# A masked two-layer attention kernel: moving the first batch's count, the last but one batch's units and statistics, and the last products and stores

## The chip, the core and the metric

The kernel runs on one core of a Trainium2 chip. A core has five engines with their own instruction queues: TensorE (PE, matrix products; PEld is its loading of weights), VectorE (DVE), ScalarE (ACT), GpSimd (POOL) and SyncE (SP), which here only issues transfers. The metric is the device time of one execution in microseconds (us).

## The reference

Sixteen graphs of 1024 nodes with 256 features pass two layers of masked multi-head attention, each behind a normalization without weights and a ReLU, and each with a residual. The first layer has 4 heads of 64, the second 8 heads of 32.

```python
# x: (16, 1024, 256) float32, adj: (16, 1024, 1024) int32 of 0 and 1
h = jnp.maximum(_layernorm(x, axis=-1), 0.0)
x = x + _L0_gnn_ref(h, adj, Wq, Wk, Wv, Wo, bo)     # H = 4, DK = 64
h = jnp.maximum(_layernorm(x, axis=-1), 0.0)
x = x + _L1_gnn_ref(h, adj, Wq, bq, Wk, bk, Wv, bv, Wo, bo)   # H = 8, D = 32

# in a layer
scores = jnp.einsum('bhne,bhme->bhnm', Q, K) * scale
scores = jnp.where(mask, scores, -jnp.inf)
attn = jax.nn.softmax(scores, axis=-1)
heads = jnp.einsum('bhnm,bhme->bhne', attn, V)
concat = heads.transpose(0, 2, 1, 3).reshape(...)
return concat @ Wo.T + bo
```

## The kernel before

**Steps.** Scores are computed transposed: keys on the partitions, queries along the free axis. A *step* handles four blocks of 128 keys by 512 queries. Its pieces are `scores` (L457, four products into two PSUM pairs `ps`), `exponentials` (for each pair of blocks L480 on DVE, which brings in the mask, and L486 on ACT, the exponential), and `weigh` (L498, products of the exponentials `p` with the values, gathered in `po`). A *group* is half of the heads for one half of the queries (`qh` 0 or 1, `g` 0 or 1): 4 steps in layer 0, 8 in layer 1. A batch so has 16 steps in layer 0 and 32 in layer 1, and there are 768 in all. The order is layer 0 of batch 0, and then always layer 0 of batch b+1 followed by layer 1 of batch b; at the end stands layer 1 of the last batch. Below, `a` is the first step of a batch's layer 0, `c` the first step of the layer 1 that follows it (for the last but one batch step 704), and `e` = `c` + 32 the first step of the last batch's layer 1.

**The stream.** `Stream.run` walks the steps, two at a time in layer 0 and one at a time in layer 1. `weigh` of a step comes two steps after its scores (`LEAD`). All other work is put at a step with `later(step, function, ...)`. Within a step the order is: the scores, `weigh`, the counts, the exponentials, then what is due there in the order in which it was put, and last the *units*, which are large pieces of TensorE work. They are `k` and `q` (L273), `values` (L309) and `end_half` (L439), sixteen 256-column or eight 512-column instructions each. On an even step of layer 1 that has a unit, `weigh` is left to the next step:

```python
if wide == 2 or i % 2 or not self.large(i):
    for _, st in waiting:
        weigh(st)
```

Each engine runs its instructions in program order, so this walk is also the order in each queue.

**The sums of the softmax.** Sums over the keys are made by adding `p` tiles first and then multiplying with ones on TensorE (`count`, L350, into the one bank `pz`). In layer 0 `add_tiles` adds the tiles of two steps (L507 and L510 on DVE or POOL, L511 and L513 on POOL), and `count_added` counts at the end of the query half. In layer 1 POOL adds pairs of steps (L611), and some sums are added by transfers (L595). An odd step's `p` tile has only two buffers, an even one's seven; the reader that frees the odd ones is L510 or L611. `spread` copies the sums to SBUF (L369, ACT) and sends them with four transfers to `sums` (L382, SP). `invert` takes reciprocals (L390, DVE) and stores them (L392, SP). `fetch` reads them back spread out (L401, SP), and `normalize` scales `cat` with them (L409, POOL). `copy_out` (L361, ACT) has filled `cat` from `po`, and frees the one `po` bank. `end_half` multiplies `cat` with the output weights into `py` (L439) and adds the result to `x` (L444, DVE); in layer 1 it stores `x` as well (L447, SP). `test` (L295, DVE) folds the sums into a verdict on their range.

All of `ps`, `pq`, `pv` and `py` take turns in three PSUM pairs, so a product waits for the reader of the third one before it.

**The next layer's inputs.** `norms` puts `stats` at two steps (L198 and L199 on DVE; at the second of them also L202 to L208 on POOL), `norm` at two more (L217, ACT) and `add_bias` (L226, POOL). `block_inputs` puts `turn_blocks` (L243, DVE), a store (L248) and four loads (L255) on SP, and the units `k`, `q` and `values`.

**The end.** The very last group is in a hurry: `finish` scales the last half of the heads itself, in two halves of the queries (L420 and L421, DVE), multiplies (L424), adds (L430) and stores with eight transfers (L432, SP). Behind it stand the verdict (L838 to L842), its load into every engine (L1019) and a branch around a careful version that is not taken here (L1020).

Of the kernel before, what the change touches and what calls it, by code (L numbers as in the profile page):

```python
# [18 lines left out]
P = 128  # L19
# [71 lines left out]
def fast_program(ctx, tc, a, w, loads, chk):  # L91
# [3 lines left out]
    nc = tc.nc  # L95
    x, adj, out = a["x"], a["adj"], a["out"]
    B, N, E = x.shape
# [18 lines left out]
    def psum_pair(name):  # L116
        return ps_s.tile([P, 2, 512], F32, tag="ps_s", name=name)
# [3 lines left out]
    def quarters(of, b, half):  # L121

        rows = of[b].rearrange("(t h p g) e -> h g p t e", h=QH, p=32, g=4)[half]
        return [rows[g] for g in range(4)]

    def by_tile(cols):

        return cols.rearrange("p (g t q) -> p t g q", g=4, q=32)

    def tiled(cols):  # L130

        return cols.rearrange("p (t g q) -> p t g q", g=4, q=32)
# [186 lines left out]
    class Group:  # L319
# [91 lines left out]
        def finish(self):  # L411

            inp, qh = self.inp, self.qh
            inv = work.tile([P, 512], F32, tag="inv", name=f"inv_{self.n}")
            py = psum_pair(f"py_{self.n}").rearrange("p a (t e) -> p (a t) e", e=E)
            rows, cat = xs[inp.b, qh], self.half.cat
            dst = quarters(out, inp.b, qh)
            for h in range(2):
                q = ts(h, 256)
                nc.vector.reciprocal(tiled(inv)[:, ts(h, 2)], by_tile(self.s)[:, ts(h, 2)])  # L420
                nc.vector.tensor_mul(cat[:, self.g, q], cat[:, self.g, q], inv[:, q])  # L421
                for i in (2 * h, 2 * h + 1):
                    for c in range(2):
                        nc.tensor.matmul(  # L424
                            py[:, i, :], cat[:, c, ts(i, P)], w.o[self.layer][:, c, :],
                            start=(c == 0), stop=(c == 1),
                        )
            for h in range(2):
                t = ts(h, 2)
                nc.vector.tensor_add(rows[:, t, :], py[:, t, :], rows[:, t, :])  # L430
                for g in range(4):
                    nc.sync.dma_start(dst[g][:, t, :], rows[ts(g, 32), t, :])  # L432

        def end_half(self):
            inp, qh = self.inp, self.qh
# [88 lines left out]
    class Stream:  # L524
# [12 lines left out]
        def later(self, i, f, *args):  # L537
            self.due.setdefault(i, []).append((f, args))
# [101 lines left out]
        def end_group(self, i, gr):  # L640

            if gr.hurry:
                for f in (gr.spread, gr.finish, gr.inp.test):
                    self.later(i, f)
                return

            if gr.layer == 0:
                if gr.g == 0:
                    gr.half.first = gr
                    return  # L650
                self.later(i + 3, gr.count_added)
                at = (3, 4, 5, 7, 11) if gr.qh else (3, 5, 6, 7, 11)
                if gr.inp.b == B - 1 and gr.qh:
                    at = 3, 4, 5, 7, 13
                if gr.inp.b == 0:
                    at = (3, 5, 5, 6, 8) if gr.qh else (3, 5, 6, 7, 9)
            else:
                at = ((6, 12, 15, 19), (8, 12, 14, 17, 19), (6, 9, 11, 14), None)[2 * gr.qh + gr.g]
                if gr.pairs:
                    at = 2, 5, 6, 7, 9  # L660
                elif gr.last:
                    at = 4, 6, 7, 9, 11
            for k, f in zip(at, (gr.spread, gr.invert, gr.fetch, gr.normalize)):
                self.later(i + k, f)
            if gr.last:

                k = 7 if gr.layer or gr.inp.b == 0 else 25 if gr.inp.b == B - 1 else 37
                self.later(i + k, gr.inp.test)
            if gr.g == 1:
                self.later(i + at[4], gr.end_half)  # L670
# [79 lines left out]
    def norms(inp, half, *at, whole=False, bias=None):  # L750

        for i, f in zip(at, (inp.stats, inp.stats, inp.norm, inp.norm)):
            rest = (whole,) if i in at[2:] else ()
            later(i, f, half, (0, 1) if i in (at[0], at[2]) else (2, 3), *rest)
        later(at[3] + 1 if bias is None else bias, inp.add_bias, half)

    def half_inputs(inp, half, *at):

        for i, f in zip(at, (inp.turn, inp.k, inp.q, inp.values)):
            later(i, f, half)  # L760

    def block_inputs(inp, half, turn, put, place, *at):

        later(turn, inp.turn_blocks, half)
        later(put, inp.put_blocks, half)
        later(place, inp.place_blocks, half)
        for i, f in zip(at, (inp.k, inp.q, inp.values)):
            later(i, f, half)
# [9 lines left out]
    for t in range(NT):  # L778
        i = 7 + 2 * t
# [8 lines left out]
    for b in range(B - 1):  # L788
        mine, a, c = inputs[1][b], first[b + 1], second[b]
        if b == 0:  # L790

            norms(mine, 0, a + 4, a + 6, a + 7, a + 8, whole=True)
            half_inputs(mine, 0, a + 10, a + 12, a + 13, a + 14)
            norms(mine, 1, a + 10, a + 11, a + 12, a + 13, whole=True)
            half_inputs(mine, 1, a + 15, c, c + 6, c + 2)
        else:
            norms(mine, 0, a - 20, a - 16, a - 15, a - 13, bias=a)
            block_inputs(mine, 0, a - 10, a - 8, a - 4, a, a + 2, a + 8)
            norms(mine, 1, a - 14, a - 10, a - 8, a - 6, bias=a + 6)
            block_inputs(mine, 1, a, a + 6, a + 7, c, c + (6 if b + 2 < B else 8), c + 2)  # L800
        for i, u in zip((0, 2, 4, 6, 7, 9, 11, 13), range(NT)):
            later(a + i, masks[b].second, u)
        if b + 2 < B:
            other, mask = inputs[0][b + 2], masks[b + 2]
            later(a + 6, open_x, b + 2, 0)
            later(c, open_x, b + 2, 1)
            if b == 0:
                norms(other, 0, a + 12, a + 14, c, c + 1, bias=c + 34)
                block_inputs(other, 0, c + 2, c + 3, c + 4, c + 8, c + 16, c + 18)
                norms(other, 1, c + 3, c + 4, c + 6, c + 7, bias=c + 36)  # L810
                block_inputs(other, 1, c + 8, c + 9, c + 12, c + 22, c + 26, c + 30)
            else:
                norms(other, 0, a + 10, a + 12, a + 13, a + 15, bias=c + 34)
                block_inputs(other, 0, c, c + 1, c + 2, c + 8, c + 16, c + 18)
                norms(other, 1, c + 2, c + 4, c + 5, c + 6, bias=c + 36)
                block_inputs(other, 1, c + 7, c + 8, c + 12, c + 22, c + 26, c + 30)
            at = 5, 8, 10, 12, 14, 45, 49, 51, 53
            for t in range(NT):
                later(a + at[t], mask.load, t)
                later(a + at[t + 1], mask.put, t)  # L820
                later(a + at[t + 1] + (1 if t == 4 else 2), mask.flip, t)
        else:
            last, e = inputs[1][b + 1], c + 32
            norms(last, 0, c + 8, c + 10, c + 11, c + 12)
            block_inputs(last, 0, c + 14, c + 15, c + 16, c + 20, c + 22, c + 26)
            norms(last, 1, c + 18, c + 19, c + 20, c + 21)
            block_inputs(last, 1, c + 24, c + 25, c + 26, e, e + 8, e + 2)
            for i, u in zip((4, 8, 12, 16, 18, 20, 24, 28), range(NT)):
                later(c + i, masks[b + 1].second, u)
    stream.run()  # L830
# [156 lines left out]
def kernel(  # L987
# [28 lines left out]
    with ExitStack() as fast, tc.manual_schedule():  # L1016
        fast_program(fast, tc, a, w, loads, chk)
# [61 lines left out]
```

## Time and profile before

| | |
|---|---|
| Median of 3 runs | 3116.97 us (3116.34 to 3117.56) |
| The profiled execution's own time | 3117.3 us |
| Its span, first to last instruction | 3115.5 us |
| PE busy | 3092.8 us (99%), 16724 instructions |
| DVE busy | 2478.7 us (80%), 2754 |
| ACT busy | 2243.3 us (72%), 2440 |
| POOL busy | 2354.3 us (76%), 1358 |
| Mean granted clock of TensorE | 0.998 |
| L480, one instruction | 1215 ns, x1536 |
| L486, one instruction | 1056 ns, x1536 |
| L611, one instruction | 2428 ns, x510 |

Busy time is the sum over an engine's instructions, and the share is that of the span. A row of a timeline gives start, duration, engine, line, operation, what it writes and reads, and how many instructions were merged; in brackets follow the engine's idle time before it and the instruction that ended it. A row of the waits gives who waited for whom: us in total, times, longest. A row of busy time in a stretch gives the stretch, its length, the busy time of PE, PEld, DVE, ACT and POOL with instruction counts, the granted clock (1.00 is full speed), the share of the transfer engines and GB/s. Starts are us from the start of the span.

### The profile page before, as it was taken

Reading aid. Unit: us, or ns where it says so; the run is one execution under the profiler, and the core shown is the slowest. Engines: PE = TensorE matmul, PEld = TensorE weight load, DVE = VectorE, ACT = ScalarE, POOL = GpSimd, SP = SyncE. Lnnn points to the kernel's source line nnn. Section 1 sums busy time; section 2 is a strip of 40 time slices with the busy share of each in tenths; the row PEclk is TensorE's granted clock in tenths of the full one; section 3 lists DMA queues with packets and bytes.
Section 4 is the critical chain, followed back from the end, with each engine's and each line's share of the span. In section 5 each row is a group of like instructions: output and inputs, shape, how many; then the busy total and the mean of one; then the engine's idle time right before and its main releaser. Section 6 shows DMA issues by size and latency. Waiting matters only on the chain.

```text
span 3115.5 us, 45742 instructions
## 1 busy us (share of the span) xinstructions
PE 3092.8 (99%) x16724; PEld 1221.2 (39%) x16724; DVE 2478.7 (80%) x2754; ACT 2243.3 (72%) x2440; POOL 2354.3 (76%) x1358
## 2 busy tenths in 40 slices
PE   9999999999999999999999999999999999999998
PEld 4443433434334343433434434343343433434333
DVE  5778787887878888788887878878788787887776
ACT  6667767777677767777777677777777767776775
POOL 3568778787877868778687786877868788786876
PEclk9999999999999999999999999999999999999999
DMA  4224545454463544535445463554545545453331
GB/s 132 58 69 113 129 106 123 121 112 118 102 140 110 119 119 101 139 103 116 122 101 138 106 129 99 116 129 103 126 116 112 123 109 122 121 111 82 78 73 33
DMA packets 259224, 341.28 MB, mean 110 GB/s; under 512 B 58288, under 2 KB 218288, under 8 KB 241968
## 3 DMA queue, kind: packets, MB, share of 16 engines
q0 software_dynamic: 19152, 139.47, 22.8%
q1 hardware_dynamic: 239840, 198.82, 22.0%
q8 instruction: 133, 2.18, 0.3%
q14 instruction: 99, 0.81, 0.1%
HBM read 149.95 MB, written 47.96 MB: 64 GB/s over the span
## 4 chain that ended last, share of the span: by engine, by line
PE 94%; DVE 1%; SPq 1%; DMA 1%; ACT 1%; issue 1%; POOL 0%; ACTq 0%; DVEq 0%; POOLq 0%
PE ps L457 32%; PE po L498 29%; PE pq L273 14%; PE pv L309 7%; PE py L439 7%; PE pz L350 4%; DVE p L480 1%; SPq L382 0%; DMA sums<-s 0%; SPq L152 0%; DMA inv<-vd 0%; ACT p L486 0%; POOL p L611 0%; DVE x L444 0%; PE py L424 0%
## 5 line engine op out<-in xcount | busy, mean ns | idle before, releaser
L486 ACT ACTIVATE p<-p 128x1024 f32<-128x1024 f32 x1536 | 1614.2, 1056 | 663.0 <-DVE p L480 599.4
L480 DVE SCALAR_TENSOR_TENSOR p<-mask,ps 128x1024 f32<-128x1024 fp8e5 x1536 | 1787.5, 1215 | 379.4 <-PE ps L457 369.1
L611 POOL TENSOR_TENSOR p<-p,p 128x1024 f32<-128x1024 f32 x510 | 1212.6, 2428 | 176.8 <-PE po L498 176.7
L457 PE MATMUL ps<-qT,kT 32*128 32x512 f32 (+1 forms) x6144 | 1097.5, 628 | 3.9 <-DVE p L480 2.0
L498 PE MATMUL po<-p,v 128*32 128x512 f32 (+1 forms) x6144 | 978.6, 600 | 1.7 <-ACT cat L361 1.5
L457 PEld LDWEIGHTS ps<-qT,kT 32*128 32x128 f32 (+1 forms) x6144 | 371.0, 184 | 660.0 <-issue 313.8
L498 PEld LDWEIGHTS po<-p,v 128*32 128x32 f32 (+1 forms) x6144 | 233.4, 118 | 680.7 <-issue 486.6
L511 POOL TENSOR_TENSOR p<-p 128x1024 f32<-128x1024 f32 x128 | 302.6, 2364 | 142.2 <-DVE p L510 136.9
L510 POOL TENSOR_TENSOR p<-p,p 128x1024 f32<-128x1024 f32 x64 | 150.9, 2358 | 199.8 <-DVE p L507 179.6
L409 POOL TENSOR_TENSOR cat<-cat,inv 128x512 f32<-128x512 f32 x127 | 175.6, 1388 | 99.8 <-DMA inv<-vd 99.4
L439 PE MATMUL py<-wo,cat 128*128 128x256 f32 x1008 | 236.4, 388 | 2.7 <-POOL cat L409 1.5
L309 PE MATMUL pv<-wv,hT 128*128 128x256 f32 x1024 | 237.7, 385 | 0.0
L273 PE MATMUL pq<-hT,wk 128*128 128x512 f32 x512 | 236.7, 605 | 0.0
L273 PE MATMUL pq<-hT,wq 128*128 128x512 f32 x512 | 236.6, 605 | 0.0
L439 PEld LDWEIGHTS py<-wo,cat 128*128 128x128 f32 x1008 | 187.4, 191 | 77.8 <-issue 23.5
L309 PEld LDWEIGHTS pv<-wv,hT 128*128 128x128 f32 x1024 | 189.4, 190 | 71.7 <-issue 15.1
L507 DVE TENSOR_TENSOR p<-p 128x1024 f32<-128x1024 f32 x128 | 172.6, 1349 | 0.0
L595 POOL DMA_DIRECT2D p<-p x133 | 122.6, 922 | 55.4 <-POOL p L611 26.8
L350 PE MATMUL pz<-p,ones 128*32 128x512 f32 x1248 | 163.1, 596 | 0.0
L361 ACT COPY cat<-po 128x512 f32<-128x512 f32 x128 | 73.4, 573 | 116.7 <-PE py L439 96.6
L444 DVE TENSOR_TENSOR x<-py,x 128x1024 f32<-128x1024 f32 x63 | 77.2, 1225 | 99.7 <-PE py L439 98.8
L226 POOL TENSOR_TENSOR x<-x,bo 128x1024 f32<-128x1024 f32 x64 | 155.7, 2504 | 0.0
(52 smaller groups left out, 1667.2 us busy)
## 6 DMA issues: line engine op xcount, KB each, us to landing
p<-p POOLq DMA_DIRECT2D x133, 1024.0 KB, 7.8
adj<-in_adj_dram SPq DMA_DIRECT2D x512, 128.0 KB, 3.0
turned<-hn SPq DMA_DIRECT2D x58, 512.0 KB, 3.8
hT<-turned SPq DMA_DIRECT2D x232, 128.0 KB, 3.0
x<-in_x_dram SPq DMA_DIRECT2D x128, 128.0 KB, 3.0
inv<-vd SPq DMA_DIRECT2D x128, 128.0 KB, 3.0
inv<-vd SPq DMA_DIRECT2D x252, 64.0 KB, 3.0
out_dram<-x SPq DMA_DIRECT2D x124, 128.0 KB, 2.2
```

The source lines that it names most:

```text
L273: nc.tensor.matmul(pq[:, m, :], wt[self.layer][:, c, ts(m, P)], self.hT[half][:, c, :], start=(c == 0), stop=(c == 1),)
L309: nc.tensor.matmul(pv[:, i, :], self.hT[half][:, c, ts(i, P)], w.v[self.layer][:, c, :], start=(c == 0), stop=(c == 1),)
L350: nc.tensor.matmul(self.s[ts(r, 32), :], w.ones.to_broadcast([P, 32]), of, start=start, stop=stop)
L409: nc.gpsimd.tensor_mul(o, o, inv)
L439: nc.tensor.matmul(py[:, i, :], self.half.cat[:, c, ts(i, P)], w.o[self.layer][:, c, :], start=(c == 0), stop=(c == 1),)
L457: nc.tensor.matmul(st.ps[i // 2][:, i % 2, :], gr.inp.kT[r * D : (r + 1) * D, gr.g, ts(kt, P)], gr.inp.qT[gr.qh][r * D : (r + 1) * D, gr.g ...
L480: nc.vector.scalar_tensor_tensor(out=half, in0=gr.mask.m[gr.qh][:, kt // 4, :, kt % 4].unsqueeze(1).to_broadcast([P, 2, 512]), scalar=-EDG ...
L486: nc.scalar.activation(half, half, AF.Exp, scale=gr.scale)
L498: nc.tensor.matmul(gr.o[r * D : (r + 1) * D, :], gr.inp.v[:, kt, h * D : (h + 1) * D], st.halves[i // 2][:, i % 2, :], start=(kt == 0), st ...
L507: nc.vector.tensor_add(a, a, b)
L511: nc.gpsimd.tensor_add(a, a, b)
L611: nc.gpsimd.tensor_add(half, half, of)
```

## The change

Four things are edited, and the arithmetic stays the same.

1. In `finish` the four products with the first group's half of `cat` are issued ahead of the scaling of the second half; the products with the second half follow each scaling. The start and stop marks now stand on the first and the last product of a PSUM bank. Of the eight last stores every second one is issued by ACT.
2. In batch 0, layer 0, second query half: `count_added` and `spread` one step sooner, `invert` two steps, `fetch` and `normalize` one step. With steps taken in twos, `count_added`, `spread`, `invert` and `fetch` so move to the pair of steps before, and `normalize` stays in its pair (22 and 23), but on its first step, ahead of that pair's `add_tiles`. `end_half` stays.
3. In the layer 1 of the last but one batch: the `end_half` of the last batch's layer 0 moves from c+14 to c+18, and `q` of its own second half from c+8 to c+10.
4. For the last batch's layer 1: statistics of its first half from c+8 and c+10 to c+6 and c+8. Of its second half: statistics from c+18 and c+19 to c+20 and c+22, norm from c+20 and c+21 to c+23 and c+24 (`add_bias` with it from c+22 to c+25), turn, store and loads each two steps later, and `q` from e+8 to e+10.

```diff
@@ finish
+            def product(i, c):
+                nc.tensor.matmul(
+                    py[:, i, :], cat[:, c, ts(i, P)], w.o[self.layer][:, c, :],
+                    start=c == 0 and i % 2 == 0, stop=c == 1 and i % 2 == 1,
+                )
+
+            for i in range(4):
+                product(i, 0)
             for h in range(2):
                 q = ts(h, 256)
                 nc.vector.reciprocal(tiled(inv)[:, ts(h, 2)], by_tile(self.s)[:, ts(h, 2)])
                 nc.vector.tensor_mul(cat[:, self.g, q], cat[:, self.g, q], inv[:, q])
                 for i in (2 * h, 2 * h + 1):
-                    for c in range(2):
-                        nc.tensor.matmul(
-                            py[:, i, :], cat[:, c, ts(i, P)], w.o[self.layer][:, c, :],
-                            start=(c == 0), stop=(c == 1),
-                        )
+                    product(i, 1)
...
-                    nc.sync.dma_start(dst[g][:, t, :], rows[ts(g, 32), t, :])
+                    queue = nc.scalar if g % 2 else nc.sync
+                    queue.dma_start(dst[g][:, t, :], rows[ts(g, 32), t, :])
@@ end_group
-                self.later(i + 3, gr.count_added)
+                early = gr.inp.b == 0 and gr.qh
+                self.later(i + (2 if early else 3), gr.count_added)
                 at = (3, 4, 5, 7, 11) if gr.qh else (3, 5, 6, 7, 11)
                 if gr.inp.b == B - 1 and gr.qh:
-                    at = 3, 4, 5, 7, 13
+                    at = 3, 4, 5, 7, 17
                 if gr.inp.b == 0:
-                    at = (3, 5, 5, 6, 8) if gr.qh else (3, 5, 6, 7, 9)
+                    at = (2, 3, 4, 5, 8) if gr.qh else (3, 5, 6, 7, 9)
@@ the order of the work, b >= 1
-            block_inputs(mine, 1, a, a + 6, a + 7, c, c + (6 if b + 2 < B else 8), c + 2)
+            block_inputs(mine, 1, a, a + 6, a + 7, c, c + (6 if b + 2 < B else 10), c + 2)
...
-            norms(last, 0, c + 8, c + 10, c + 11, c + 12)
+            norms(last, 0, c + 6, c + 8, c + 11, c + 12)
             block_inputs(last, 0, c + 14, c + 15, c + 16, c + 20, c + 22, c + 26)
-            norms(last, 1, c + 18, c + 19, c + 20, c + 21)
-            block_inputs(last, 1, c + 24, c + 25, c + 26, e, e + 8, e + 2)
+            norms(last, 1, c + 20, c + 22, c + 23, c + 24)
+            block_inputs(last, 1, c + 26, c + 27, c + 28, e, e + 10, e + 2)
```

## The prediction

> **What bounds the kernel now.** I read the page first: TensorE (PE) is busy 3092.8 of 3115.5 us, so all that an edit of the order can win is PE's idle time, its slow clock, and the tail after the last matmul. Then I asked which waits PE has in the whole run:
>
> ```profile
> PE py L424 <- DVE cat L421: 2.3, 1, 2.3
> ...
> PE py L439 <- DVE p L480: 1.2, 1, 1.2
> ```
>
> The first is the tail's. The second lies at 2927 us, and near it lies most of what the lines left out hold of scores (L457) that wait for L480, 2.0 us in 6 waits, and of po (L498) for the copy L361, 1.5. Two waits of py on POOL's scaling (L409), 1.5 in all, are batch 0's, at 160 us. These are the three places of the change. Next the busy time in stretches of 3.41 us, laid on the two places where the granted clock is half:
>
> ```profile
> 2924.39:2927.80 3.41, 1.38 (x7) 0.49 (x6) 2.31 (x3) 3.41 (x6) 3.41 (x2) 0.99 0.30 60
> 2927.80:2931.22 3.42, 3.42 (x9) 2.71 (x9) 3.17 (x3) 2.96 (x3) 3.17 (x2) 0.51 0.02 5
> 2941.45:2944.87 3.42, 2.13 (x19) 0.47 (x17) 3.42 (x4) 3.42 (x5) 3.19 (x2) 1.00 0.54 153
> 3098.47:3101.88 3.41, 1.08 (x5) 0.67 (x4) 3.02 (x3) 0.27 (x1) 0.00 (x0) 0.99 0.03 2
> 3101.88:3105.29 3.41, 3.41 (x9) 2.67 (x9) 1.26 (x2) 0.00 (x0) 0.00 (x0) 0.51 0.00 0
> ```
>
> After the bounds come PE's busy us and, third from the right, the clock. Stretches with 1.38 and 1.08 us of PE are each followed by one at half clock; one with 2.13 is not (nor is one with 1.96 at 20 us). So a stall costs a second time. Last the timeline of each place.
>
> **The tail.**
>
> ```profile
> 3098.16 0.70 PE L424 MATMUL py<-wo,cat 128*128 128x256 f32 x2
> ...
> 3101.19 4.95 PE L424 MATMUL py<-wo,cat 128*128 128x256 f32 x14 [2.33 <-DVE cat L421]
> ...
> 3106.17 1.29 DVE L430 TENSOR_TENSOR x<-py,x 128x512 f32<-128x512 f32 x2 [3.00 <-PE py L424]
> ```
>
> and, from the answer on line 1020, the branch at the end:
>
> ```profile
> L1020 PEldq COMPARE_BRANCH  x1: 4455/4455/4455, 3109.3 to 3109.3; - x1
> ```
>
> Each product is two instructions of some 0.215 us at full clock (the 16 of L439 take 3.65 us: 0.23 each). The change issues all four first-group products (8 instructions) at 3098.16, until about 3100.05, in what was idle time. After the first scaling (3101.19) come 4 instructions, until 3102.1; the last 4 wait for the second scaling (ends 3103.18) and run 3103.29 to 3104.31. The stretch 3098.47 to 3101.88 then has 1.58 + 0.67 = 2.25 us of PE instead of 1.08, above the 2.13 that kept the clock, so I take no half clock: L430 starts at 3104.33 and not 3106.17, 1.84 sooner. If it stays at half, the last 4 take 1.9 us: 1.0 sooner. The Trainium skill (TensorE: Matmul & The Clock Gate, "Why this matters for your kernels") says that gaps over some 3 us are to be avoided; by that a gap of 2.33 is harmless, the 14 instructions would keep their 4.95 / 14 = 0.354 us, and the last 4 end at 3104.7: 1.45. The row of 0.51 decides: 1.84.
>
> Behind it SP issues 8 stores from 3106.89, 4.48 us in all, the last with 1.22; only then its load of the verdict (3111.4) and the waits for the stores. With four on ACT, idle there, each queue needs 4 x 0.43 = 1.7 us. No ACT-issued transfer is in the trace, so its cost is bounded by the same issue on SP (0.43, landing 1.7 to 4.1 us) and by one from POOL (0.92, landing 7.8); I take SP's, the same kind of issue. But L1020's branch on PE, started by the verdict at 3109.3, ends at 3113.71 whatever SP does, and the span ends 1.8 us later; SP's last wait is about 3114.5. So of SP's 2.8 us only some 0.75 comes out. The skill (DMA: Bandwidth & Descriptors, "Rules for kernel authors") holds that spreading over queues saves issue time only. Read alone that gives 4.48 - 1.7 = 2.8; the branch's row leaves 0.75. Tail: -1.84 - 0.75 = **-2.6** (-1.0 to -4.5; with ACT's landing at 7.8 the stores gain becomes a loss of about 1).
>
> **Batch 0** (steps 20 to 28):
>
> ```profile
> 153.91 2.37 POOL L510 TENSOR_TENSOR p<-p,p 128x1024 f32<-128x1024 f32 x1
> ...
> 156.31 2.35 DVE L480 SCALAR_TENSOR_TENSOR p<-mask,ps 128x1024 f32<-128x1024 fp8e5 x2 [0.85 <-POOL p L510]
> ...
> 164.58 1.22 DVE L444 TENSOR_TENSOR x<-py,x 128x1024 f32<-128x1024 f32 x1 [0.94 <-PE py L439]
> ```
>
> L510 frees the buffer that L480 of step 25 writes; the scaling of cat (L409, 2.51 us) came after it, at 158.70. The count (1.0 us of PE) moves from 139.58 to about 128.7; its sums are final at 124.0, so it waits for nothing, and PE's total at 144 is unchanged. The copy (0.59 on ACT), four sum transfers (2.4 on SP, behind an adjacency load that ends at 133), reciprocal (0.25), one store and four inverse loads (2.4, behind the next adjacency load) follow one pair of steps sooner and land near 150; the x load behind them on SP issues some 1.3 us later, for a batch that is not yet read. So the scaling is ready. It now stands ahead of L510 on POOL: 153.95 to 156.45. The products need not wait (0.94 + 0.53 = 1.47 of idle, with the issue around it 1.77: end 162.7). But L510 ends at 158.8, so L480 of step 25 starts there, 2.5 late. Two waits vanish behind it: L295 and L507 took 1.45 and 2.34 us while POOL scaled, 0.45 and 1.2 elsewhere. DVE: 158.85 + 2.35 + 0.45 + 1.2 + 1.25 = 164.1 for L444, against 164.58. The next scores' third block takes its PSUM buffer from L444 and then follows DVE, which has no idle time until 182.7. So 0.5 and not 1.77: **-0.5** (-1.8 if DVE catches up; +1.0 if L507 stays at 2.34).
>
> **Last but one batch.** c is its first layer-1 step (2874.21), e = c+32. Three rules from the rows: a step's scores take 1.07 us or end 1.16 after the first L480 of the step before (L480 ended 2918.23, scores 2919.39); an odd step's L480 waits for the POOL sum of the step four earlier:
>
> ```profile
> 2924.01 1.22 DVE L480 SCALAR_TENSOR_TENSOR p<-mask,ps 128x1024 f32<-128x1024 fp8e5 x1 [1.67 <-POOL p L611]
> ...
> 2927.61 5.41 PE L439 MATMUL py<-wo,cat 128*128 128x256 f32 x16 [1.19 <-DVE p L480]
> ...
> 2943.86 1.06 PE L498 MATMUL po<-p,v 128*32 128x512 f32 x8 [1.29 <-ACT cat L361]
> ```
>
> and a unit (8 or 16 matmuls, 3.65 us) on an even step defers that step's po products to the next. Followed through:
> - Statistics at c+6 put 1.31 us of DVE ahead of the L480 of c+7: scores of c+8 end at 2907.2, not 2905.84. Those at c+8 put another 1.31 ahead of c+9; q, now at c+10, runs 2913.3 to 2916.9. The scores of c+12 start at 2920.7 against 2917.75: 3.0 lost.
> - Their POOL part (1.9 us) now precedes the two scalings, which waited 1.83 for a transfer until 2912.87: ending at 2915.4, not 2914.1. It no longer stands at 2919.74 before L611. c+12 to c+17 have no unit now: scores of c+13 start at 2922.8, c+15 2927.5, c+17 2934.0. Before, c+17 started at 2938.80 with the 3.65 unit behind it: 2934.0 + 3.65 = 2937.65, 1.2 ahead.
> - Then POOL is late again: the sums of c+13 end at 2936.7 and 2939.1, L480 of c+17 waits for both, and py at c+18 starts at 2940.4 after 1.3 idle. The worst 3.41 us before it has about 2.0 of PE, near the 1.96 that kept the clock: no half clock, by a little. py ends 2944.0; the 1.29 wait for the copy (L361) is hidden under it. Scores of c+19 start 0.8 ahead of 2944.85.
> - The later statistics of half 1 free ACT at c+20, and the 0.26 that PE waited for L287 goes. Turn, store and four loads move two steps on SP, landing near 2986 for k at about 2988: covered by 2 us, and if not, at most 2 us are lost. add_bias at c+25 fits POOL's 3.06 of idle. q from e+8 to e+10 swaps equal steps: 0.
> - c+27's scores: 2973.2 against 2974.50. The same rules put the old ones at 2974.1, so I count the nearer **-1.0**. Bounds: +1.5 with a half clock at c+18 (1.76, partly swallowed as before), -2.8 if the 1.3 idle isn't there.
>
> **Sum**: -2.6 - 0.5 - 1.0 = -4.1 on the profiled 3117.3 gives 3113.2; the median of the runs is 0.3 lower, so 3112.9.
>
> **Rivals.** (1) *Each stall simply goes*: -3.4, -1.8, -2.8, together -8.0: 3109.0. For it: each wait named is the one moved. Against: DVE and POOL have no slack in two of the places. (2) *The gains are given back*: the clock stays half in the tail (-1.0), batch 0 and the stretch give 0: 3116.0. (3) *Slower: POOL's debt in the eight steps c+10 to c+18 without a unit*. Four pairs of sums (18.9) with two scalings (2.6), statistics (1.9), two accumulates (2.4) and a bias (2.5) are 28.3 us against four pairs of steps at 5.36 (21.4): 6.9 of debt, and the two odd-step buffers absorb one pair, 5.4. If more than that is uncovered, each pair costs as the worst one before, 2920.38 to 2932.95 less a unit: 8.9 against 5.4, 3.5 lost. Four such are 14, less the 5.5 lost there now, plus 1.8 of half clock: +10.3; with the tail and batch 0, +7.2: 3124.2.
>
> **Numbers.** 0.2% is 6.2 us, about what a measurement of this kernel can tell from no change. My forecast 0.62 (own range 3110.8 to 3115.0), rival 1 0.17, rival 2 0.15, rival 3 0.06. Faster is rival 1, same the forecast and rival 2, slower rival 3. The range 3109.0 to 3116.9 leaves out part of rival 1's far side and rival 3.
>
> **What would show it.** Tail: 8 instructions of py from 3098, the clock of the next 3.4 us full, L430 about 1.8 us after the second L421's start, four stores on each of SP and ACT. Batch 0: no py wait, L480 waiting some 3.3 us for L510. Last but one batch: py at c+18 with about 1.3 us of idle on L480. Wrong if the clock is half at c+18 or in the tail, if L444 in batch 0 is not where DVE stands, or if the end waits for a store from ACT.

## The result, and the profile after

The changed kernel is slower: a median of 3122.02 us (3120.50 to 3123.59 over 20 runs) beside 3116.32 us of the kernel before (3114.24 to 3118.64 over 20 runs). The ratio is 1.0018, with an interval of 1.0012 to 1.0025: 5.7 us more, where 4.1 less were forecast. The profiled execution of the changed kernel took 3121.75 us, and its span is 3120.0.

In the changed kernel the lines behind `finish` have a number 6 higher, and those behind `end_group` 7: L480 is now L486, L457 L463, L498 L504, L611 L617, L439 L445, and the branch L1020 is L1027. In `finish` itself L424, L421 and L430 became L420, L430 and L435. Lines up to L409, with the range test L295, kept theirs.

First the page, then PE's waits in the whole run (who waited for whom: us in total, times, longest):

```profile
span 3120.0 us, 45743 instructions
...
PE 3097.7 (99%) x16724; PEld 1220.7 (39%) x16724; DVE 2481.5 (80%) x2754; ACT 2243.8 (72%) x2440; POOL 2351.5 (75%) x1358
```

```profile
PE ps L463 <- DVE p L486: 5.8, 8, 1.8
...
PE py L420 <- DVE cat L430: 1.9, 2, 1.0
...
PE py L445 <- DVE p L486: 1.2, 1, 1.2
```

PE has the same 16724 instructions as before and 4.9 us more of busy time, which with the same work means a slower clock. The two waits of py on POOL's scaling in batch 0 are gone; the only one left on L409 is the tail's, of 0.2 us. The wait of py on the last p of its half has the same 1.2 us at its new place. The new thing is the first line: scores wait for L486 8 times and 5.8 us, where it was 6 times and 2.0.

To find where, I compared the start of each step's scores in the two traces. The number is after minus before, so a fall is a gain:

| step | after minus before, us | what lies between this row and the one above |
|---|---|---|
| 19 | +0.21 | |
| 31 | -0.57 | batch 0: 0.78 gained |
| c (704) | -1.72 | unchanged code: 1.15, spread over many steps |
| c+12 | +0.74 | statistics and `q` put in earlier: 2.46 lost for now |
| c+18 | -7.54 | steps without a unit: 8.3 ahead |
| c+19 | -3.48 | `end_half`, now here: 4.06 given back |
| c+28 | -4.01 | |
| c+30 | +1.76 | **5.8 lost** |
| e+8 | +1.76 | |
| e+10 | -1.37 | `q` no longer at e+8: 3.1 ahead for now |
| e+12 | +6.39 | `q` now at e+10: **4.6 lost** against e+8 |
| last step | +6.39 | |

Behind the last step the tail gains 1.9, so the span grows by 6.39 - 1.9 = 4.5. All that is edited up to c+28 gains what was forecast or more. The loss has two places, c+29 and e+11. These are the timelines of the changed kernel around the first, DVE and then POOL (start, duration, engine, line, operation, output and inputs, how many merged; in brackets the idle time before it and what ended it):

```profile
2970.37 4.78 DVE L295 SCALAR_TENSOR_TENSOR chk<-sums,chk 128x32 f32<-128x32 f32 x2
2975.07 4.60 DVE L486 SCALAR_TENSOR_TENSOR p<-mask,ps 128x1024 f32<-128x1024 fp8e5 x4
```

```profile
2970.09 2.67 POOL L226 TENSOR_TENSOR x<-x,bo 128x1024 f32<-128x1024 f32 x1
2972.76 4.67 POOL L617 TENSOR_TENSOR p<-p,p 128x1024 f32<-128x1024 f32 x2
```

The two instructions of the range test L295, on 32 columns, take 4.78 us. In the kernel before they are at the same step and take 0.40. POOL had no sum in progress then; it was issuing a transfer (L595), which did not hold them, and after it was idle. DVE, and then POOL:

```profile
2972.98 0.40 DVE L295 SCALAR_TENSOR_TENSOR chk<-sums,chk 128x32 f32<-128x32 f32 x2
```

```profile
2972.85 0.87 POOL L595 DMA_DIRECT2D p<-p  x1 [0.30 <-POOL p L611]
2976.78 2.38 POOL L611 TENSOR_TENSOR p<-p,p 128x1024 f32<-128x1024 f32 x1 [3.06 <-PE po L498]
```

Taken one by one, the first of the two in the changed kernel runs from 2970.37 to 2972.82 and POOL's L226 ends at 2972.76; the second runs until 2975.15, and the first L617 ends at 2975.10. Each ends just behind the POOL instruction that was in progress. L486 stands behind them in DVE's queue, and PE behind L486:

```profile
2973.41 1.13 PE L463 MATMUL ps<-qT,kT 32*128 32x512 f32 x4
2976.34 1.55 PE L463 MATMUL ps<-qT,kT 32*128 32x512 f32 x4 [1.80 <-DVE p L486]
2977.82 1.94 PE L504 MATMUL po<-p,v 128*32 128x512 f32 x8
2979.68 2.09 PE L463 MATMUL ps<-qT,kT 32*128 32x512 f32 x8
```

The same group of 8 products L504 takes 1.06 us a few steps on and 1.94 here: the clock has fallen. The busy time in stretches of 3.41 us, laid on both places (bounds, length, then PE, PEld, DVE, ACT, POOL; third from the right the granted clock):

```profile
2973.49:2976.90 3.41, 1.61 (x8) 0.52 (x8) 3.41 (x3) 0.58 (x1) 3.41 (x2) 1.00 0.76 144
2976.90:2980.32 3.42, 3.42 (x16) 0.72 (x16) 2.77 (x3) 3.20 (x4) 2.19 (x3) 0.50 0.40 158
2980.32:2983.73 3.41, 3.41 (x20) 0.59 (x16) 1.85 (x2) 2.08 (x3) 3.41 (x2) 0.50 0.56 154
...
3028.09:3031.50 3.41, 1.66 (x7) 0.60 (x6) 3.41 (x4) 1.67 (x3) 1.72 (x2) 1.00 0.00 0
3031.50:3034.91 3.41, 3.41 (x6) 1.31 (x4) 1.69 (x2) 2.78 (x3) 0.00 (x0) 0.50 0.00 0
```

So the wait is paid a second time, in 6.83 us and in 3.41 us at half clock. The second place, e+11, from the timeline of all engines:

```profile
3023.90 4.68 POOL L617 TENSOR_TENSOR p<-p,p 128x1024 f32<-128x1024 f32 x2 [0.27 <-PE po L504]
...
3025.06 3.60 DVE L295 SCALAR_TENSOR_TENSOR chk<-sums,chk 128x64 f32<-128x64 f32 x2
3028.59 4.60 DVE L486 SCALAR_TENSOR_TENSOR p<-mask,ps 128x1024 f32<-128x1024 fp8e5 x4
3029.85 1.13 PE L463 MATMUL ps<-qT,kT 32*128 32x512 f32 x4 [1.74 <-DVE p L486]
3030.98 5.40 PE L273 MATMUL pq<-hT,wq 128*128 128x512 f32 x8
```

And the kernel before at the same step:

```profile
3023.31 0.48 DVE L295 SCALAR_TENSOR_TENSOR chk<-sums,chk 128x64 f32<-128x64 f32 x2
...
3026.85 4.71 POOL L611 TENSOR_TENSOR p<-p,p 128x1024 f32<-128x1024 f32 x2 [4.96 <-PE po L498]
```

Before, the unit `q` at e+8 left that step's po products to the next step, POOL had nothing to add until 3026.85, and the test fell into that gap. With `q` at e+10 the gap is two steps later, and the test no longer is in it.

The three places of the prediction look like this after the change. Batch 0:

```profile
154.03 2.51 POOL L409 TENSOR_TENSOR cat<-cat,inv 128x512 f32<-128x512 f32 x2
156.49 2.38 POOL L516 TENSOR_TENSOR p<-p,p 128x1024 f32<-128x1024 f32 x1
158.91 2.35 DVE L486 SCALAR_TENSOR_TENSOR p<-mask,ps 128x1024 f32<-128x1024 fp8e5 x2 [3.48 <-POOL p L516]
...
164.02 1.22 DVE L450 TENSOR_TENSOR x<-py,x 128x1024 f32<-128x1024 f32 x1
```

The last but one batch at c+18:

```profile
2935.41 1.13 PE L463 MATMUL ps<-qT,kT 32*128 32x512 f32 x4 [0.59 <-DVE p L486]
2937.72 3.72 PE L445 MATMUL py<-wo,cat 128*128 128x256 f32 x16 [1.18 <-DVE p L486]
```

And the tail, with the branch at the end:

```profile
3104.62 1.99 PE L420 MATMUL py<-wo,cat 128*128 128x256 f32 x8 [0.17 <-POOL cat L409]
...
3107.57 1.10 PE L420 MATMUL py<-wo,cat 128*128 128x256 f32 x4 [0.96 <-DVE cat L430]
...
3109.61 1.70 PE L420 MATMUL py<-wo,cat 128*128 128x256 f32 x4 [0.93 <-DVE cat L430]
3111.34 1.29 DVE L435 TENSOR_TENSOR x<-py,x 128x512 f32<-128x512 f32 x2 [1.79 <-PE py L420]
3112.06 1.76 SPq L438 DMA_DIRECT2D out_dram<-x  x4
3112.07 1.85 ACTq L438 DMA_DIRECT2D out_dram<-x  x4
```

```profile
L1027 PEldq COMPARE_BRANCH  x1: 4252/4252/4252, 3114.6 to 3114.6; - x1
```

### The profile page after: what moved, and what is told of

Same layout as the page of the kernel before. It is cut to its first block, busy times and chain, and to the rows that moved or that the text cites. A ratio compares the mean times of both kernels' runs of the same rounds, so it can differ in the third digit from the quotient of the medians.

```text
span 3120.0 us, 45743 instructions
## 1 busy us (share of the span) xinstructions
PE 3097.7 (99%) x16724; PEld 1220.7 (39%) x16724; DVE 2481.5 (80%) x2754; ACT 2243.8 (72%) x2440; POOL 2351.5 (75%) x1358
## 3 DMA queue, kind: packets, MB, share of 16 engines
q0 software_dynamic: 19152, 139.47, 22.8%
## 4 chain that ended last, share of the span: by engine, by line
PE 95%; DVE 2%; SPq 1%; issue 1%; ACT 1%; POOL 0%; DMA 0%; DVEq 0%; ACTq 0%; POOLq 0%
PE ps L463 32%; PE po L504 29%; PE pq L273 15%; PE pv L309 7%; PE py L445 7%; PE pz L350 4%; DVE p L486 1%; SPq L152 0%; DMA sums<-s 0%; ACT p L492 0%; SPq L382 0%; POOL p L617 0%; DVE x L450 0%; DVE qT L279 0%; PE ph L239 0%
## 5 line engine op out<-in xcount | busy, mean ns | idle before, releaser
L486 DVE SCALAR_TENSOR_TENSOR p<-mask,ps 128x1024 f32<-128x1024 fp8e5 x1536 | 1787.1, 1215 | 378.7 <-PE ps L463 365.5
L617 POOL TENSOR_TENSOR p<-p,p 128x1024 f32<-128x1024 f32 x510 | 1211.8, 2428 | 186.6 <-PE po L504 186.6
L463 PE MATMUL ps<-qT,kT 32*128 32x512 f32 (+1 forms) x6144 | 1101.4, 629 | 8.0 <-DVE p L486 5.8
L504 PE MATMUL po<-p,v 128*32 128x512 f32 (+1 forms) x6144 | 980.4, 601 | 0.2
L463 PEld LDWEIGHTS ps<-qT,kT 32*128 32x128 f32 (+1 forms) x6144 | 371.2, 184 | 667.6 <-issue 312.3
L504 PEld LDWEIGHTS po<-p,v 128*32 128x32 f32 (+1 forms) x6144 | 233.6, 118 | 680.2 <-issue 484.6
L516 POOL TENSOR_TENSOR p<-p,p 128x1024 f32<-128x1024 f32 x64 | 150.8, 2357 | 199.6 <-DVE p L513 181.9
L409 POOL TENSOR_TENSOR cat<-cat,inv 128x512 f32<-128x512 f32 x127 | 173.4, 1372 | 96.2 <-DMA inv<-vd 95.7
L445 PE MATMUL py<-wo,cat 128*128 128x256 f32 x1008 | 234.4, 386 | 1.2 <-DVE p L486 1.2
L445 PEld LDWEIGHTS py<-wo,cat 128*128 128x128 f32 x1008 | 186.3, 190 | 75.4 <-issue 25.9
L450 DVE TENSOR_TENSOR x<-py,x 128x1024 f32<-128x1024 f32 x63 | 77.1, 1224 | 99.5 <-PE py L445 98.5
L226 POOL TENSOR_TENSOR x<-x,bo 128x1024 f32<-128x1024 f32 x64 | 155.5, 2497 | 0.0
```

Source lines behind the costliest of these rows:

```text
L409: nc.gpsimd.tensor_mul(o, o, inv)
L445: nc.tensor.matmul(py[:, i, :], self.half.cat[:, c, ts(i, P)], w.o[self.layer][:, c, :], start=(c == 0), stop=(c == 1),)
L463: nc.tensor.matmul(st.ps[i // 2][:, i % 2, :], gr.inp.kT[r * D : (r + 1) * D, gr.g, ts(kt, P)], gr.inp.qT[gr.qh][r * D : (r + 1) * D, gr.g ...
L486: nc.vector.scalar_tensor_tensor(out=half, in0=gr.mask.m[gr.qh][:, kt // 4, :, kt % 4].unsqueeze(1).to_broadcast([P, 2, 512]), scalar=-EDG ...
L504: nc.tensor.matmul(gr.o[r * D : (r + 1) * D, :], gr.inp.v[:, kt, h * D : (h + 1) * D], st.halves[i // 2][:, i % 2, :], start=(kt == 0), st ...
L617: nc.gpsimd.tensor_add(half, half, of)
```

## The experiments

The theory: L295, which reads two operands from SBUF, cannot run while POOL adds or scales, and waits for the end of the POOL instruction in progress. The change gave POOL work at the two steps where L295 stands (`add_bias` at c+25, and the sums that `q` at e+8 had held back), so each 0.2 us instruction holds DVE for up to 2.5 us, PE waits for nearly 2, and then the clock falls. The main rival: the test is slow for another reason, and the loss comes from POOL being behind with its sums, or from the moved units as such. "Before" in brackets is the median of the kernel before in the runs of the same chip. These medians lie between 3115.82 and 3116.32, so a difference from the changed kernel's 3122.0 can be off by some 0.5 us.

**The test with one operand.** In the changed kernel two of the 32 range tests, those at c+26 and e+8, become two instructions that read and write `sums` alone. The range test of these two sets of sums is left out.

```diff
+        def test_one_input(self):
+            nc.vector.reciprocal(self.sums, self.sums)
+            nc.vector.reciprocal(self.sums, self.sums)
...
-                self.later(i + k, gr.inp.test)
+                covered = (gr.layer, gr.inp.b) in ((0, B - 1), (1, B - 2))
+                self.later(i + k, gr.inp.test_one_input if covered else gr.inp.test)
```

> The changed kernel (3122.0), but for two of its 32 range tests (first at step c+26, then at e+8) the two L295 instructions are replaced by two reciprocals in place: as many DVE instructions on as many numbers, with one SBUF operand instead of two. This leaves out the range test of those two sets of sums. Theory (POOL locks out a DVE instruction with two SBUF operands): the two reciprocals take about 0.25 us each though POOL is adding at that time, so 4.3 us of DVE at c+26 and 3.1 at e+8 go, and with them the 5.8 and 4.6 us that PE loses there and both half-clock stretches: 3111.6. Rival (the loss is POOL's debt and the longer gaps without a unit, the test only stands there): 3122, half clock still there. Second rival (any DVE instruction is held up there): 3122, the reciprocals last 2.3 us each.

Measured: 3113.64 us (3111.73 to 3115.12, 21 runs) [3115.88], ratio 0.9992 (0.9985 to 0.9999). From the timeline of POOL and of DVE at the first place (the lines are shifted again: L622 is the sum of p, L301 and L302 are the two reciprocals):

```profile
2973.36 2.69 POOL L226 TENSOR_TENSOR x<-x,bo 128x1024 f32<-128x1024 f32 x1
2976.02 4.71 POOL L622 TENSOR_TENSOR p<-p,p 128x1024 f32<-128x1024 f32 x2
```

```profile
2973.63 0.31 DVE L301 RECIPROCAL sums<-sums 128x32 f32<-128x32 f32 x1
2973.98 0.35 DVE L302 RECIPROCAL sums<-sums 128x32 f32<-128x32 f32 x1
```

Both reciprocals run in the middle of POOL's L226, and are not held. At e+8 they take 0.55 us each beside a sum. POOL does the same work as in the changed kernel, and 8.4 us are gone. So most of the loss comes neither from POOL's sums nor from the moved units, but from the two-operand instruction. The kind of operation does not explain it either: L486 is a SCALAR_TENSOR_TENSOR too, but with one operand in SBUF (`mask`) and one in PSUM. None of its 1536 in the changed kernel took longer than 1223 ns, though POOL is busy 75% of the time:

```profile
L486 DVE SCALAR_TENSOR_TENSOR p<-mask,ps x1536: 1160/1214/1223, 24.4 to 3099.3; 128x1024 f32<-128x1024 fp8e5 x192
```

The gain fell 2.0 us short of what was expected. In the profiled execution (3114.53) c+29 loses nothing and e+11 0.4 us, but the stall at c+18 was followed by 3.41 us of half clock, from 2940.29, which the profiled execution of the changed kernel does not have; more on this stall below.

**`q` back to e+8.**

```diff
-            block_inputs(last, 1, c + 26, c + 27, c + 28, e, e + 10, e + 2)
+            block_inputs(last, 1, c + 26, c + 27, c + 28, e, e + 8, e + 2)
```

> The changed kernel with q of the last batch put back from e+10 to e+8, nothing else. Theory: q's unit on the even step e+8 defers po products, and with them POOL's next sums, past the test, so L295 takes 0.2 us each again; the 4.6 us between e+9 and e+12 go, 3117.4, the loss at c+29 stays. Rival (debt): no difference at e+8 since the units are only swapped, 3122.

Measured: 3116.49 us (3114.51 to 3118.76, 13 runs) [3115.88], ratio 1.0 (0.9992 to 1.0009). L295 at e+8 is back at 218 and 226 ns, and nothing is lost at e+11. At c+26 it still takes 2457 and 2292 ns, and c+29 loses 4.2 us. This part of the change costs 3122.0 - 3116.5 = 5.5 us.

**The bias away from c+25.** `add_bias` of the last batch's second half, at c+25 in the changed kernel, goes to e+5.

```diff
-            norms(last, 1, c + 20, c + 22, c + 23, c + 24)
+            norms(last, 1, c + 20, c + 22, c + 23, c + 24, bias=e + 5)
```

> The changed kernel with the bias addition of the last batch's second half moved from c+25 to e+5, where POOL was idle 3 us; nothing else. Theory: without L226 POOL has nothing to do when the test of c+26 comes, L295 takes 0.2 us each, the 5.8 us at c+29 and the first half-clock stretch go: 3116.2. Rival (debt, or the turn moved to c+26 delays DVE): 3121 to 3122. If POOL's next sum starts before the second test instruction: in between, about 3119.

Measured: 3119.72 us (3117.63 to 3122.59, 21 runs) [3115.88], ratio 1.0011 (1.0005 to 1.0018). This expectation missed by 3.5. The mechanism did what was expected at c+26: L295 takes 150 and 193 ns, and the stretch goes through without a loss. But the loss at e+11 grew from 4.6 to 6.9 us. DVE's timeline there:

```profile
3017.40 2.35 DVE L486 SCALAR_TENSOR_TENSOR p<-mask,ps 128x1024 f32<-128x1024 fp8e5 x2 [1.45 <-PE ps L463]
3019.67 4.79 DVE L295 SCALAR_TENSOR_TENSOR chk<-sums,chk 128x64 f32<-128x64 f32 x2
3024.38 4.61 DVE L486 SCALAR_TENSOR_TENSOR p<-mask,ps 128x1024 f32<-128x1024 fp8e5 x4
```

The pair takes 4.79 us instead of 3.60, as it now arrives at the start of a POOL sum and not in the middle of one, and the half clock behind it lasts 6.83 us instead of 3.41. The two losses are not independent, so a part taken away doesn't give back its own 5.8.

**Both.** The edits of the last two experiments together.

> The changed kernel with both: q back at e+8 and the bias addition at e+5. Theory: both losses go and add up, 3122.0 - 5.8 - 4.6 = 3111.6, 0.15% under the kernel before (3116.3). Rival: 3121 to 3122.

Measured: 3112.55 us (3110.18 to 3115.07, 21 runs) [3115.88], ratio 0.9989 (0.9983 to 0.9996). The last step starts 4.06 us ahead of the kernel before, and there is no half clock ahead of the tail. The waits of PE:

```profile
PE ps L463 <- DVE p L486: 1.5, 4, 0.6
```

The 5.8 us of waits for L486 are 1.5. The same kernel on another chip, beside other kernels:

> The same kernel as a_both, beside the other two on one chip, for the comparison with a_both16 and a_move: 3112.6, within 1 us.

Measured: 3112.43 us (3110.68 to 3114.82, 13 runs) [3116.30], ratio 0.9990 (0.9982 to 0.9998). Its profiled execution was slower, 3113.85 beside 3110.83 us: here the stall at c+18 was followed by half clock from 2938.11.

**The test moved, nothing of the change undone.** If L295 is what costs, moving it out of POOL's way must do as much as undoing the two edits. The test at c+26 goes to e+4, that at e+8 to e+10.

```diff
-                k = 7 if gr.layer or gr.inp.b == 0 else 25 if gr.inp.b == B - 1 else 37
+                k = 7 if gr.layer or gr.inp.b == 0 else 35 if gr.inp.b == B - 1 else 37
+                if gr.layer and gr.inp.b == B - 2:
+                    k = 9
```

> The changed kernel with nothing of the change taken back; only the two range tests are put elsewhere: the first from c+26 to e+4, the second from e+8 to e+10, both on steps with a unit, where POOL's next sums are deferred. Theory (port): L295 takes at most 0.7 us at either place, both losses go: 3112 to 3113, as with both mended. Rival (the moved bias and unit cost by themselves): 3116 or more.

Measured: 3112.16 us (3110.41 to 3115.03, 21 runs) [3116.30], ratio 0.9988 (0.9981 to 0.9994). The pair at e+4 takes 0.89 us, and neither c+29 nor e+11 loses anything. Two tests, four instructions, in other places are worth 9.9 us.

**The test alone, in the kernel before.** The opposite: the kernel before with the one test of e+8 put at e+14, where POOL adds without a pause.

```diff
                 k = 7 if gr.layer or gr.inp.b == 0 else 25 if gr.inp.b == B - 1 else 37
+                if gr.layer and gr.inp.b == B - 2:
+                    k = 13
```

> The kernel before with one range test (two L295 instructions on 128x64 numbers, 0.22 us each in the trace of before) moved from e+8 to e+14, where POOL adds nearly without a gap and no unit stands. Nothing else, and no other step of the change. Theory: each waits for the POOL instruction in progress, up to 2.4 us, DVE is 2 to 4.5 us late, PE loses 2 to 5 with the clock: 3118 to 3121. Rival (a DVE instruction of 0.2 us costs 0.2 us wherever it stands, and the loss came from the moved units): 3116.

Measured: 3122.76 us (3118.64 to 3124.58, 15 runs) [3115.82], ratio 1.0022 (1.0014 to 1.0030). Two instructions of 0.22 us, moved by six steps and nothing else, cost 6.9 us. The timelines of DVE, POOL and PE there:

```profile
3044.68 4.49 DVE L295 SCALAR_TENSOR_TENSOR chk<-sums,chk 128x64 f32<-128x64 f32 x2
...
3049.25 4.55 DVE L480 SCALAR_TENSOR_TENSOR p<-mask,ps 128x1024 f32<-128x1024 fp8e5 x4
```

```profile
3039.73 9.35 POOL L611 TENSOR_TENSOR p<-p,p 128x1024 f32<-128x1024 f32 x4 [3.22 <-PE po L498]
```

```profile
3050.46 2.08 PE L457 MATMUL ps<-qT,kT 32*128 32x512 f32 x4 [2.73 <-DVE p L480]
3052.47 1.94 PE L498 MATMUL po<-p,v 128*32 128x512 f32 x8
```

POOL's four sums end at 3049.08, and the second L295 ends with the last of them. PE waits 2.73 us and is then at half clock for 6.83. This single edit has the sign of the whole change, and in these traces it costs 6.3 us from e+14 to the last step, where the two places of the change cost 5.8 and 4.6.

**Each part alone, in the kernel before.** The tail: `finish` of the changed kernel, nothing else.

> The kernel before with the change's finish alone (first-group products ahead, stores on SP and ACT). The prediction says -2.6. From the changed kernel's trace, where first product to last instruction is 15.4 us against 17.3: 1.9 to 2.0 less, so 3114.0. Rival (stores on ACT give nothing since the branch on PE ends the run): 1.3 less, 3114.6.

Measured: 3114.80 us (3112.11 to 3116.49, 13 runs) [3115.82], ratio 0.9997 (0.9989 to 1.0005). The sign fits, but the interval holds no change: not settled by the times.

Batch 0: the `early` count and `at = (2, 3, 4, 5, 8)`, nothing else.

> The kernel before with the edits of batch 0 alone (count and spread at +2, then 3, 4, 5). The prediction says -0.5; the changed kernel's trace has step 31 at 0.8 less than at step 19. 3115.1. Rival (the scaling ahead of L510 costs DVE as much as PE wins): 3115.9, no difference.

Measured: 3115.73 us (3114.55 to 3119.36, 13 runs) [3115.82], ratio 1.0001 (0.9993 to 1.0010): too small for the times. The trace shows it: the steps stand at -0.05 us at step 23 and at -0.83 at step 31, 0.8 gained, as in the changed kernel.

The last two batches, without the two edits that meet the test:

```diff
-                    at = 3, 4, 5, 7, 13
+                    at = 3, 4, 5, 7, 17
...
-            block_inputs(mine, 1, a, a + 6, a + 7, c, c + (6 if b + 2 < B else 8), c + 2)
+            block_inputs(mine, 1, a, a + 6, a + 7, c, c + (6 if b + 2 < B else 10), c + 2)
...
-            norms(last, 0, c + 8, c + 10, c + 11, c + 12)
+            norms(last, 0, c + 6, c + 8, c + 11, c + 12)
...
-            norms(last, 1, c + 18, c + 19, c + 20, c + 21)
-            block_inputs(last, 1, c + 24, c + 25, c + 26, e, e + 8, e + 2)
+            norms(last, 1, c + 20, c + 22, c + 23, c + 24, bias=e + 5)
+            block_inputs(last, 1, c + 26, c + 27, c + 28, e, e + 8, e + 2)
```

> The kernel before with the edits of the last two batches alone, with q of the last batch left at e+8 and the bias addition at e+5, so that both range tests stay out of POOL's way. The prediction says -1.0 for this part. From the trace with both mended, whose steps are 1.8 us ahead at c and 4.1 at c+31: -2.3, 3113.6. Rival (the eight steps without a unit cost as much as the rest wins; part of that 1.8 and 4.1 is drift from execution to execution): 3115.9.

Measured: 3116.64 us (3112.41 to 3118.39, 13 runs) [3115.82], ratio 1.0001 (0.9993 to 1.0009). The 3113.6 expected was missed, and its 13 runs scatter over 6 us, where the 13 of the version with both mended on the same chip lie within 4.1. The profiled execution is one of the two lowest, at 3112.63, and has gained 2.1 us from c to the end. What the others may have had shows in py at c+18. These are two executions of one kernel, the version with both mended on the first chip and on the second:

```profile
2937.67 3.72 PE L445 MATMUL py<-wo,cat 128*128 128x256 f32 x16 [1.18 <-DVE p L486]
```

```profile
2938.46 5.21 PE L445 MATMUL py<-wo,cat 128*128 128x256 f32 x16 [1.18 <-DVE p L486]
```

The same 16 instructions behind the same 1.18 us of waiting take 3.72 us in one execution and 5.21 in the other, where the granted clock is half from 2938.11 to 2941.52. Eight traces here have this stall at c+18. In four the products take 3.72 us (the changed kernel, the moved bias, both mended, and this version), in the other four 5.2 to 6.6: the stall costs nothing more, or 1.5 to 2.9 us. How often it does so in the runs without a profile can't be seen, so that the scatter of this kernel comes from there is likely and not shown.

**The stall at c+18 taken away.** If that is right, a version without the wait of py must be faster and must scatter less. `end_half` goes to c+16 instead of c+18, on top of the version with both mended: the run of steps without a unit ahead of it is then two shorter, and POOL should fall less far behind.

```diff
-                    at = 3, 4, 5, 7, 17
+                    at = 3, 4, 5, 7, 15
```

> The changed kernel with q back at e+8 and the bias at e+5 (3112.6), and the last batch's layer-0 end_half at c+16 instead of c+18, so that the stretch without a unit is six steps and not eight. Theory of POOL's debt (rival 3 of the prediction, at its measured size): the 1.2 us that py waits at c+18, with the 0.6 before it, shrink, and the executions in which that stall is followed by half clock go; against that the 1.3 us wait of po for the copy at c+18 comes back. 3111.5 to 3112.5. If the spacing is worth nothing: 3113 to 3114.

Measured: 3108.49 us (3108.11 to 3110.65, 13 runs) [3116.30], ratio 0.9978 (0.9970 to 0.9986). This version beats both kernels, by 7.8 us the one before and by 13.5 the changed one. It is 3 us faster than expected. Its 13 runs lie within 2.5 us, where the 13 without this last edit lay within 4.1. From c to c+28 its trace gains 4.7 us on the kernel before; of the two executions above, the one without the half clock gains 2.3 there and the one with it 0.8. Its PE around the moved unit:

```profile
2928.87 1.58 PE L463 MATMUL ps<-qT,kT 32*128 32x512 f32 x8
2930.45 3.72 PE L445 MATMUL py<-wo,cat 128*128 128x256 f32 x16
```

There is no bracket: py waits for nothing, and the wait of po for the copy, which was expected to come back, does not. From 2926 to 3094 us PE is busy 167.5 of 168 us, at a granted clock of 1.00.

## Why the prediction was wrong, point by point

The steps of the prediction that failed are two of its shortest: "add_bias at c+25 fits POOL's 3.06 of idle" and "q from e+8 to e+10 swaps equal steps: 0". Both were costed at nothing, by looking at the engine that carries the moved work and not at who else is at that step. DVE's L295 stands at both. The material was at hand: the trace of the kernel before has this line of durations for L295 (shortest, median, longest in ns, first and last start):

```profile
L295 DVE SCALAR_TENSOR_TENSOR chk<-sums,chk x64: 174/217/1197, 158.6 to 3107.6; 128x32 f32<-128x32 f32 x32, 128x64 f32<-128x64 f32 x32
```

An instruction of fixed shape with a median of 217 ns and a longest of 1197 waits for something that no bracket names. The prediction even used it in batch 0, where it noted that L295 and L507 took 1.45 and 2.34 us (the first for its pair) while POOL scaled, and less elsewhere. It did not ask where else those instructions stand. The Trainium skill states the rule behind it (SBUF — State Buffer, "SBUF: two separate sides"): a DVE instruction with two SBUF inputs and a GpSimd instruction that reads SBUF share one pair of ports under a lock for the whole instruction, and the other one fully blocks. The runs agree: 2.2 to 2.5 us with two inputs behind POOL (1.3 where L295 came in the middle of a sum), 0.31 to 0.55 with one input beside it.

By the prediction's own parts:

- *Tail, -2.6.* Measured -1.9: the right sign and mechanism, too large. The eight first-group products, the two groups of four and the four stores on each queue came as said, and so did the branch: L1027, started by the verdict, sets the end with 4252 ns, and the stores with what lies behind them gave about 0.7, near the 0.75 reckoned: from L435 to the end it is 8.7 us after and 9.4 before. The term that was mis-sized is the 1.84. From the first product to L435 it is 6.72 us after and 8.01 before, 1.3 gained. The clock did not stay full: it is half from 3110.0, and the last four products take 1.70 instead of 1.10. That lies between the 1.84 and the prediction's own lower case of 1.0. The prediction laid its stretch of 3.41 us where the kernel before had it; in this execution the stretch ahead of the half clock is 3106.62 to 3110.03, with 1.52 us of PE. In other executions the clock did stay full, as predicted: six of the nine traces here with the new `finish` have the last products at full clock. From the start of the last step to the end these nine take 22.8 to 23.7 us, and the four with the old `finish` 23.8 to 25.2, on average 1.7 more.
- *Batch 0, -0.5.* Measured -0.8. The scaling runs ahead of L516, L486 waits 3.48 us for it (3.3 said), py waits for nothing, and DVE sets when L450 comes, as argued.
- *Last but one batch up to c+27, -1.0.* Measured against step c: -2.3. The walk through the steps holds: 2.5 lost at c+12 (3.0 said), 5.8 ahead at c+18, py there with 1.18 of idle on L486 (1.3 said) and no half clock in this execution, 1.8 ahead at c+19 (0.8 said). The statistics cost somewhat less than reckoned. That the clock stays full at c+18 was "by a little"; four of the eight traces with this stall show that it can go the other way.
- *Between batch 0 and c* the code is the same and the steps came out 1.15 us sooner. The runs of one kernel differ by more than that, so nothing is read from it.

Together up to c+28, and with the tail, the parts are -0.8 - 2.3 - 1.9 = -5.0. This split is read from the traces and not settled by the times: the medians of the three parts run alone add up to -1.0 - 0.1 + 0.8 = -0.3, each with an interval of some 2.5 us to either side. The kernel with the two edits mended has a median 3.3 us below the kernel before: near the -4.1 forecast. What the sum lacked is the 5.8 + 4.6 = 10.4 us at c+29 and e+11, for which it had 0.

Of the rivals, the third had the right sign for the wrong reason. Its debt of POOL was to decide between c+10 and c+18, and there PE was ahead by 5.8 us. A small part of it is real: the waits for L486 at c+18, and `end_half` two steps sooner takes them away and gives 4 us. But the loss of the change is not there. The first rival, that each stall simply goes, was put at 3109.0; the last version reaches 3108.5, with two places of the change mended and one unit two steps sooner.

## What to carry to other kernels

Where work is moved on or onto POOL, list what DVE does at the same steps and mark each instruction that reads two operands from SBUF: its length there was what was left of the POOL instruction in progress, whatever its own size. A step costed at zero because the engine had idle time needs the question who used that idle time. Such a collision can be undone from either side, and moving the small instruction is the cheaper one: four instructions elsewhere gave as much here as undoing both edits.

## What the hardware showed that was not expected

- Two 0.22 us instructions in another place cost 6.9 us of 3116 (each took 2.2 us, PE waited 2.73, and the half clock followed), in a kernel whose PE is 99% busy.
- The wait repeats for every instruction: when POOL has several in its queue, each L295 of a pair waits for the end of one of them, so that the pair took 4.78 and 3.60 us at the two places of the changed kernel, and 4.79 and 4.49 in two others.
- Each half-clock stretch ahead of the last products lasts 3.41 us or twice that, and within a trace every change of the clock lies on one grid of 3.41 us. Where this grid lies differs from one execution to the next, and the same 1.18 us stall so cost nothing more, or 1.5 to 2.9 us. It stands in twelve traces: at c+18 in eight, and at c+14 in the four that leave `end_half` there. In the five that kept the full clock the products behind it start 1.4 to 2.2 us after a mark of the grid; in the seven with half clock they start 2.4 to 3.3 us after one, or 0.3 to 1.0. No run set this on purpose.
- PE's busy time in the stretch ahead, by which the prediction judged, does not decide it. Stretches with 1.61 and 1.66 us of PE were followed by half clock and one with 2.23 at c+18 was not, which fits its reading. But stretches with 1.97 (the version with both mended, second chip), 2.13 (the test with one operand) and 2.58 (the moved tests) were followed by half clock, and in the tail ones with 1.50 (batch 0 alone) and 1.70 (the moved tests) were not. What decides is left open, and so is why the half clock lasts one stretch or two.
